# Turning nine blocks of tokens on VectorE, and moving maxima, router and entries among the key pairs

## The chip, the cores and the metric

The kernel runs on one core of one Trainium2 chip. The metric is the device time of one execution in microseconds (us), the median of several runs. A difference within 0.2% is about what can't be told from no change here.

## The reference

One layer on x of 4096 tokens by 256, all in float32: causal attention with one head, then a mixture of experts, each behind a layer norm and each added to x.

```python
x = x + attn(layernorm(x))      # softmax(mask(Q K^T / 16)) V, causal, S = 4096, D = 256
h = layernorm(x) @ W_in + b_in
probs = softmax(h @ W_gate + b_gate)          # 8 experts, the best 2 of each token
mid = relu(einsum('nd,edh->neh', h, W1) + b1) # hidden size 1024
moe = sum over a token's 2 experts of share * (mid @ W2 + b2)
x = x + moe @ W_out + b_out
```

## The kernel before

**Blocks of tokens.** The tokens are cut in eight blocks of 512 (`b`, `TB`), each of four tiles of 128, and in sixteen groups of 256 queries (`g`, two a block). `xb[b]` holds x of a block in SBUF from the first load to the end; attention is added to it in place, later b_out.

**Turning.** A matrix product on TensorE wants the channel on the partitions. So each block is turned twice: its normalized rows before attention (`z`, made by `ln_rows(0, b)`, turned into `zT[b]`), and its normalized rows after attention (`z1`, turned into `z1T`). `turn` (L263) does this with eight transposes of 128x128 on TensorE (line 268) into two banks of PSUM, and two copies of 128x512 out of them by VectorE (line 274). `squares` (L804) is another way that the kernel already has, for the rows of the experts: sixteen of VectorE's own 32-wide transposes straight from SBUF to SBUF (line 810).

**Attention.** `project(b)` makes qT of a block (`pq`) and `values(b)` its V with a column of ones (`pv`). `scores(g)` computes for each of the g+1 key pairs `c` (256 keys each) the scores of 256 queries (`ps`, line 484). ScalarE copies them out (line 493), VectorE keeps a running maximum over the pairs (`mx`, line 499). After the last pair, `top` is turned (`pt`, line 520), reduced to `m`, spread again (`pmax`, line 527), and then VectorE subtracts it from each pair (line 531) and ScalarE takes the exponential in place. `attend(g)` multiplies the result with the values (`po`, line 549), in two banks for the two tiles of 128 queries. Then VectorE divides by the sum (`rinv`, line 559), adds to x and takes the statistics for the second norm.

**The order in the loop.** Iteration g issues `scores(g + 1)` ahead of `attend(g)`, so that exponentials of the next group run beside the products of this one. At the first group of a block b the loop also prepares z of block b+1 and lets block b-1 enter the experts: `enter(b - 1)` turns z1, multiplies it with W_in and the gate (`ph`, line 291), and writes the rows to DRAM; `route(b - 1)` finds the two best experts on VectorE by a chain of some twenty small operations, counts tokens with two products on TensorE (`pk`, lines 349 and 352), and scatters the token's number into the expert's list in DRAM (`slots`, line 367, by GpSimd). At the end of `route`, GpSimd adds b_out to x of the block (line 386). The last block's first group (g = 14) differs: `enter(6)` stands inside `scores(15)` after `BETWEEN` pairs, and `plan` and `route(6)` follow.

**The experts.** Work items (full blocks `a` and `b` of 256 entries, halves `c`, quarters in pairs `d`, a late one `z`) fetch their slots, rows and weights some items ahead, multiply with W1 (`pm`) and W2 (`pe`), and scatter to `parts`. At the end the two parts of each token are added, multiplied with W_out (`pa`, `pf`) and added to x.

**Order.** A planner places the instructions of each engine by their data and their place in the source; `tc.keep_in_program_order` ties single ones to the order of the source. Each engine executes its own list in order. PSUM has four banks for scores and other products (`ps_mm`), two for `ps_tr`, two for sums (`ps_o`). SP's queue issues loads and stores, POOL's the indirect ones.

**The beginning.** Five products of zeros run while the first loads arrive (line 112). Q and K weights are turned and multiplied with each other (`pqk`, line 419); between the two halves of that product stands `turn` of block 0.

Of the kernel before, what the change touches and what calls it, by code (L numbers as in the profile page):

```python
# [26 lines left out]
TOPK = 2  # L27
SQ = 32
LATE = 2
USUAL = 6  # L30
BETWEEN = 6
# [4 lines left out]
def preln_attention_moe_kernel(  # L36
# [51 lines left out]
    dram = ctx.enter_context(tc.tile_pool(name="dram", bufs=1, space=bass.MemoryType.DRAM))  # L88
    psum = ctx.enter_context(tc.tile_pool(name="psum", bufs=1, space=bass.MemoryType.PSUM))
# [13 lines left out]
    slots = dram.tile([NE * R, 1], I32, name="slots")  # L103
# [6 lines left out]
    pw = ps_mm("warm")  # L110
    for _ in range(5):
        done = nc.tensor.matmul(
            pw[:, :QB],
            lhsT=zeros,
            rhs=zeros.unsqueeze(1).to_broadcast([P, QB // P, P]),
            start=True,
            stop=True,
        )
        tc.keep_in_program_order(done)
# [4 lines left out]
    def load_square(w, name, queue=nc.sync):  # L124
        t = const.tile([P, ND, w.shape[1]], F32, tag=name, name=name)
        queue.dma_start(out=t, in_=w.rearrange("(c p) e -> p c e", p=P))
        return t

# [6 lines left out]
    kw_sb = load_square(Kw, "kw", nc.scalar)  # L135
    qw_sb = load_square(Qw, "qw", nc.scalar)
# [104 lines left out]
    def ln_shift(k, b, tiles=TPB):  # L241
        s = ts(b, tiles)
        mv, rstd, shift = lns[k]
        nc.vector.scalar_tensor_tensor(
            shift[:, s, :], mv[:, s, 0:1], -1.0, rstd[:, s, :], ALU.mult, ALU.mult
        )

    def ln_rows(k, b, pool, tiles=TPB):

        mv, rstd, shift = lns[k]  # L250
        zs = []
        for j in range(TPB):
            t = b * TPB + j
            if t % tiles == 0:
                ln_shift(k, t // tiles, tiles)
            z = pool.tile([P, D], F32, tag=f"z{k}", name=f"z{k}_{t}", bufs=TPB)
            nc.vector.tensor_scalar(
                z, xb[b][:, j, :], rstd[:, t, :], shift[:, t, :], ALU.mult, ALU.add
            )
            zs.append(z)  # L260
        return zs

    def turn(k, b, zs, zT, first=False):  # L263

        for c in range(ND):
            pt = ps_mm(f"pz{k}_{b}_{c}")
            for j in range(TPB):
                done = nc.tensor.transpose(pt[:, ts(j, P)], zs[j][:, ts(c, P)], ident)
                if first:
                    tc.keep_in_program_order(done)  # L270
            if first and c:
                nc.scalar.copy(zT[:, c, :], pt)
            else:
                nc.vector.tensor_copy(zT[:, c, :], pt)
# [6 lines left out]
    def enter(b, zs, pool):  # L281

        zT = pool.tile([P, ND, TB], F32, tag="z1T", name=f"z1T{b}", bufs=1)
        turn(1, b, zs, zT)
# [3 lines left out]
        for j in range(TPB):  # L288
            ph = ps_mm(f"ph{b}_{j}")
            for c in range(ND):  # L290
                nc.tensor.matmul(
                    ph[:, :DG],
                    lhsT=zT[:, c, ts(j, P)],
                    rhs=win_sb[:, c, :],
                    start=(c == 0),
                    stop=(c == ND - 1),
                )
            nc.vector.tensor_tensor(lg[:, j, :], ph[:, D:DG], bgate_bc, ALU.add)
            nc.vector.tensor_tensor(hr[:, j, :], ph[:, :D], bin_bc, ALU.add)
# [12 lines left out]
    def route(b, lg, seen, pool):  # L312
# [34 lines left out]
        pk = ps_o(f"pk{b}")  # L347
        pkv = pk[:, : TPB * NE]
        nc.tensor.matmul(
            pkv, lhsT=before, rhs=both.rearrange("p t e -> p (t e)"), start=True, stop=False  # L350
        )
        nc.tensor.matmul(
# [6 lines left out]
        for k in range(TOPK):  # L359
# [6 lines left out]
            for j in range(TPB):  # L366
# [3 lines left out]
                    in_=assign[:, b * TPB + j, k : k + 1],  # L370
# [10 lines left out]
        for k in range(TOPK):  # L381
# [3 lines left out]

        nc.gpsimd.tensor_tensor(
            xb[b], xb[b], bout_bc.unsqueeze(1).to_broadcast([P, TPB, D]), ALU.add
        )
# [3 lines left out]
    attn = ctx.enter_context(tc.tile_pool(name="attn", bufs=1))  # L392
# [11 lines left out]
    def prepare_scores(between):  # L404

        wT = {}
        for name, w in (("qwT", qw_sb), ("kwT", kw_sb)):
            wT[name] = attn.tile([P, ND, D], F32, tag=name, name=name)
            pt = ps_tr(f"p{name}")
            for h in range(ND):  # L410
                for c in range(ND):
                    nc.tensor.transpose(pt[:, ts(h * ND + c, P)], w[:, c, ts(h, P)], ident)
            nc.scalar.copy(wT[name].rearrange("p h d -> p (h d)"), pt)
# [54 lines left out]
    def scores(g, between=None):  # L468


        b, q = divmod(g, QPB)
        ss, mx = [], None
        top = attn.tile([P, QB], F32, tag="top", name=f"top{g}", bufs=2)
        for c in range(g + 1):
            if between is not None and c == BETWEEN:
                between()
# [15 lines left out]
            if c < g:  # L492
# [3 lines left out]
                else:  # L496
                    old = mx
                    mx = attn.tile([P, TB], F32, tag="mx", name=f"mx{g}_{c}", bufs=2)
                    nc.vector.tensor_tensor(mx, ps, old, ALU.max)  # L499
# [13 lines left out]
            for u in range(1, KU):  # L513
                nc.vector.tensor_tensor(
                    top[:, u * P :], top[:, u * P :], s[:, u, u * P :], ALU.max
                )

        pt = ps_tr(f"pt{g}")
        for u in range(KU):
            nc.tensor.transpose(pt[:, ts(u, P)], top[:, ts(u, P)], ident)  # L520
        m = attn.tile([P, KU], F32, tag="m", name=f"m{g}", bufs=2)
        nc.vector.tensor_reduce(
            m, pt[:, :QB].rearrange("p (u k) -> p u k", k=P), AX.X, ALU.max
        )
        pm = ps_tr(f"pmax{g}")
        for u in range(KU):
            nc.tensor.transpose(pm[:, ts(u, P)], m[:, u : u + 1].to_broadcast([P, P]), ident)  # L527
        for c in range(g + 1):
            s = ss[c]
            if c < g:  # L530
                nc.vector.tensor_tensor(  # L531
                    s, s, pm[:, :QB].unsqueeze(1).to_broadcast([P, KU, QB]), ALU.subtract
                )
                nc.scalar.activation(s, s, AF.Exp)  # L534
                continue
            for u in range(KU):
                nc.vector.tensor_tensor(
                    s[:, u, u * P :], s[:, u, u * P :], pm[:, u * P : QB], ALU.subtract
                )
                nc.scalar.activation(s[:, u, u * P :], s[:, u, u * P :], AF.Exp)  # L540
        return ss

    def attend(g, ss):
        po = [ps_o(f"po{g}_{u}") for u in range(KU)]
        for c in range(g + 1):
            for k in range(KU):
                kt = c * KU + k
                for u in range(k if c == g else 0, KU):
# [6 lines left out]
                    )  # L555
        for u in range(KU):
# [109 lines left out]
    def take_late():  # L666
# [8 lines left out]
        where = slots[ds(at, SB), :].rearrange("(p u) o -> p (u o)", u=SU)  # L675
# [29 lines left out]
    def fetch_rows(item):  # L705
# [8 lines left out]
        for j in range(parties):  # L714
# [9 lines left out]
                in_=slots[ds(at, su * rest), :].rearrange("(p u) o -> p (u o)", u=su),  # L724
# [25 lines left out]
    def fetch_weights(item, homes=None):  # L750
# [3 lines left out]
        sets, c2 = [], attn.tile([P, D], F32, tag="z0", name=f"c2_{k}{m}", bufs=TPB)  # L754
# [49 lines left out]
    def squares(to, of):  # L804


        for f in range(P // SQ):
            for q in range(P // SQ):
                pin(
                    nc.vector.transpose(  # L810
                        to[ts(f, SQ)][..., ts(q, SQ)], of[ts(q, SQ)][..., ts(f, SQ)]
                    )
                )

    def turn_rows(item, h):
# [4 lines left out]
        squares(  # L820
            hT.rearrange("p c (u s) -> p c u s", u=su),
            h.rearrange("p u (c f) -> p c u f", c=ND),
        )
# [115 lines left out]
    first_rows = ln_rows(0, 0, attn, 1)  # L939
    prepare_scores(lambda: turn(0, 0, first_rows, zT[0], True))  # L940
# [11 lines left out]
    for e in range(NE):  # L952
# [11 lines left out]
    assign = const.tile([P, NT, TOPK], I32, tag="assign", name="assign")  # L964
    nc.gpsimd.iota(assign, [[TOPK * P, NT], [1, TOPK]], base=0, channel_multiplier=TOPK)
    empty = attn.tile([P, NE * R // P], I32, tag="s", name="empty", bufs=NS)
    nc.gpsimd.memset(empty, NONE)
    nc.sync.dma_start(out=slots.rearrange("(p n) o -> p (n o)", p=P), in_=empty)
# [4 lines left out]
        out=rows[TOPK * (S - TB) :, :].rearrange("(t p) d -> p t d", p=P),  # L973
        in_=zero.unsqueeze(1).to_broadcast([P, TOPK * (TPB + 1), D]),
    )

    row = scores(0)
    values(0)
    prepare_biases()
    for g in range(NT // KU):  # L980
        b, q = divmod(g, QPB)
        coming = q == 0 and b + 1 < NB
        lg = []

        def send():
            lg.append(enter(b - 1, rows1, attn))


        last = q == 0 and b == NB - 1
        nxt = None  # L990
        if g + 1 < NT // KU:
            nxt = scores(g + 1, send if last else None)
        if coming:
            ahead = ln_rows(0, b + 1, attn)
        if last:
# [3 lines left out]
            seen = route(b - 1, lg[0], seen, attn)  # L999
            got, hTs = {}, {}  # L1000
            for n in range(AHEAD + 1):
                got[n] = fetch_rows(work[n])
            for n in range(AHEAD):
                got[n] += fetch_weights(work[n])
            weighed = AHEAD
        elif q == 0 and b > 0:
            send()
        if coming:
            turn(0, b + 1, ahead, zT[b + 1])
        attend(g, row)  # L1010
        row = nxt
        if coming:
            project(b + 1)
            values(b + 1)
        if lg and not last:
            seen = route(b - 1, lg[0], seen, attn)
        if q == QPB - 1:
            ln_rstd(1, b)
            if b + 2 < NB:
                stats0(b + 2)  # L1020
            rows1 = ln_rows(1, b, attn)
# [77 lines left out]
    for n, item in enumerate(work):  # L1099
# [13 lines left out]
        while weighed < len(work) and sum(map(sets_of, work[n : weighed + 1])) <= HOMES:  # L1113
# [3 lines left out]
            weighed += 1  # L1117
        following = None
        if n + 2 < len(work):
            following, behind = hidden(work[n + 1], got[n + 1], hTs.pop(n + 1), behind)  # L1120
        if n == 0:
            lg = enter(NB - 1, rows1, attn)
# [71 lines left out]
```

## Time and profile before

| what | value |
|---|---|
| median of 3 runs | 1090.61 us (1090.59 to 1092.51) |
| profiled execution: its time, its span | 1100.16 us, 1098.4 us |
| mean granted TensorE clock | 0.995 |
| TensorE (PE) busy | 1080.9 us, 98% |
| VectorE (DVE) busy | 689.2 us, 63% |
| ScalarE (ACT) busy | 331.9 us, 30% |
| GpSimd (POOL) busy | 238.1 us, 22% |
| attention, about | to 588 us |
| experts and last product, about | from 588 us |

The page is of one execution. Each row of a group of instructions gives its line, engine, operation, out<-in with shapes and the number of records, then busy time, mean duration in ns, and the idle time just before with what ended it. A float32 product appears as two records on PE, a transpose as one. Durations of neighbouring instructions can overlap, so what one costs its engine is read from start to start.

### The profile page before, as it was taken

The numbers are of one execution on the slowest core, as the hardware profiler recorded it, in microseconds if no ns is written. First come the engines' busy times: TensorE is split into PE (matmuls) and PEld (weight loads), VectorE is DVE, ScalarE is ACT, GpSimd is POOL, SyncE is SP. The second block draws the span as 40 slices with busy tenths as digits, with TensorE's granted clock in tenths as the row PEclk, the third lists the DMA queues.
The fourth block names the chain that finished last, engine by engine and source line by source line (L and its number), as shares of the span: only waits on it lengthen the run. The fifth ranks groups of instructions, "written<-read, shape, count | busy, mean of one in ns | idle before, by whom it ended". The sixth has DMA issues, their size and how long they took to land. (4 is left out here: it accounts for less than half of the span.)

```text
span 1098.4 us, 15700 instructions
## 1 busy us (share of the span) xinstructions
PE 1080.9 (98%) x5077; PEld 894.7 (81%) x5077; DVE 689.2 (63%) x2134; ACT 331.9 (30%) x731; POOL 238.1 (22%) x292
## 2 busy tenths in 40 slices
PE   7999999999999999999999989999999999999998
PEld 5878888888888888888888878687877777777887
DVE  4678576583673556346392643767778876868636
ACT  1323232332341423233132122232322332324244
POOL 2023211202102010201322412323232231313110
PEclk8999999999999999999999999999999999999999
DMA  8010101010001001001085465696969797979285
GB/s 265 2 40 1 39 0 39 1 39 1 1 1 39 1 1 39 1 1 39 4 260 174 133 187 186 222 337 220 339 209 351 233 330 219 339 214 316 99 289 190
DMA packets 114888, 148.34 MB, mean 135 GB/s; under 512 B 23149, under 2 KB 94770, under 8 KB 114804
## 3 DMA queue, kind: packets, MB, share of 16 engines
q1 hardware_dynamic: 105876, 129.70, 36.2%
q0 software_dynamic: 8384, 17.09, 4.6%
q8 instruction: 41, 0.67, 0.3%
q10 hardware_dynamic: 544, 0.52, 0.1%
q14 instruction: 43, 0.35, 0.1%
HBM read 124.79 MB, written 22.75 MB: 134 GB/s over the span
## 5 line engine op out<-in xcount | busy, mean ns | idle before, releaser
L549 PE MATMUL po<-v,s 128*128 128x257 f32 x1056 | 237.4, 380 | 1.1 <-DVE rinv L559 1.1
L484 PE MATMUL ps<-qT,zT 128*128 128x256 f32 x1088 | 233.0, 374 | 0.0
L484 PEld LDWEIGHTS ps<-qT,zT 128*128 128x128 f32 x1088 | 203.0, 190 | 27.8 <-issue 0.5
L549 PEld LDWEIGHTS po<-v,s 128*128 128x128 f32 x1056 | 197.3, 190 | 28.0 <-issue 1.5
L493 ACT COPY s<-ps 128x512 f32<-128x512 f32 x120 | 70.2, 585 | 192.8 <-PE ps L484 140.1
L843 PE MATMUL pm_a<-hT_a,w_a 128*128 128x256 f32 x544 | 122.0, 383 | 2.9 <-ACT mid_a L852 2.9
L910 PE MATMUL pe_a<-w_a,mid_a 128*128 128x256 f32 x544 | 121.6, 380 | 0.0
L843 PEld LDWEIGHTS pm_a<-hT_a,w_a 128*128 128x128 f32 x544 | 104.4, 192 | 17.8 <-ACT mid_a L852 3.3
L910 PEld LDWEIGHTS pe_a<-w_a,mid_a 128*128 128x128 f32 x544 | 102.6, 190 | 19.0 <-issue 5.6
L367 POOL DMA_INDIRECT slots<-assign,ati x64 | 62.5, 977 | 254.8 <-DVE ati L365 236.4
L852 ACT ACTIVATE mid_a<-pm_a,c_a 128x256 f32<-128x256 f32 x136 | 63.9, 472 | 171.0 <-PE pm_a L843 144.9
L499 DVE TENSOR_TENSOR mx<-ps,mx 128x512 f32<-128x512 f32 x91 | 62.8, 690 | 83.0 <-ACT s L493 61.5
L534 ACT ACTIVATE s<-s 128x512 f32<-128x512 f32 x120 | 71.7, 629 | 59.5 <-DVE s L531 59.2
L810 DVE STREAM_TRANSPOSE hT_a<-h_a 32x128 f32<-32x128 f32 x272 | 82.2, 302 | 6.3 <-issue 2.5
L531 DVE TENSOR_TENSOR s<-s,pmax 128x512 f32<-128x512 f32 x120 | 73.0, 679 | 4.9 <-PE pmax L527 4.9
L919 POOL DMA_INDIRECT parts<-y_a,slot_a x34 | 34.0, 1001 | 170.0 <-DVE y_a L918 149.9
L810 DVE STREAM_TRANSPOSE mid_c<-raw_c 32x256 f32<-32x256 f32 x128 | 55.8, 436 | 1.9
L910 PE MATMUL pe_b<-w_b,mid_b 128*128 128x256 f32 x256 | 56.8, 380 | 0.0
L843 PE MATMUL pm_b<-hT_b,w_b 128*128 128x256 f32 x256 | 56.6, 379 | 0.0
L910 PEld LDWEIGHTS pe_b<-w_b,mid_b 128*128 128x128 f32 x256 | 48.5, 190 | 9.4 <-issue 2.8
L843 PEld LDWEIGHTS pm_b<-hT_b,w_b 128*128 128x128 f32 x256 | 48.6, 190 | 6.6
L852 ACT ACTIVATE mid_b<-pm_b,c_b 128x256 f32<-128x256 f32 x64 | 30.1, 470 | 63.0 <-PE pm_b L843 62.2
(280 smaller groups left out, 1211.4 us busy)
## 6 DMA issues: line engine op xcount, KB each, us to landing
w_a<-in_L_ffn_W_dram SPq DMA_DIRECT2D x68, 512.0 KB
w_d<-in_L_ffn_W_dram SPq DMA_DIRECT2D x48, 512.0 KB
w_c<-in_L_ffn_W_dram SPq DMA_DIRECT2D x32, 512.0 KB
w_b<-in_L_ffn_W_dram SPq DMA_DIRECT2D x32, 512.0 KB
rows<-hr SPq DMA_DIRECT2D x16, 512.0 KB
yp<-parts SPq DMA_DIRECT2D x14, 512.0 KB
x<-in_L_attn_x_dram SPq DMA_DIRECT2D x7, 512.0 KB
out_dram<-ot SPq DMA_DIRECT2D x14, 256.0 KB
```

What stands on the lines that cost most here:

```text
L367: put = nc.gpsimd.indirect_dma_start(out=slots, out_offset=bass.IndirectOffsetOnAxis(ap=ati[:, j : j + 1], axis=0), in_=assign[:, b * TPB ...
L484: nc.tensor.matmul(ps[:, u * QB + lo : (u + 1) * QB], lhsT=zT[kt // TPB][:, d, ts(kt % TPB, P)], rhs=qT[b][:, d, q * QB + lo : (q + 1) * Q ...
L493: nc.scalar.copy(flat, ps)
L499: nc.vector.tensor_tensor(mx, ps, old, ALU.max)
L531: nc.vector.tensor_tensor(s, s, pm[:, :QB].unsqueeze(1).to_broadcast([P, KU, QB]), ALU.subtract)
L534: nc.scalar.activation(s, s, AF.Exp)
L549: nc.tensor.matmul(po[u][:, : D + 1], lhsT=ss[c][:, k, ts(u, P)], rhs=vb[kt // TPB][:, kt % TPB, :], start=(kt == 0), stop=(kt == g * KU + u),
L810: nc.vector.transpose(to[ts(f, SQ)][..., ts(q, SQ)], of[ts(q, SQ)][..., ts(f, SQ)])
L843: nc.tensor.matmul(pm[:, :SB], lhsT=w1[c][:, ts(f, P)], rhs=hT[:, c, :], start=(c == 0), stop=(c == ND - 1),)
L852: nc.scalar.activation(mid[f // 2][:, f % 2, :], pm[:, :SB], AF.Relu, bias=c1[:, f : f + 1])
L910: nc.tensor.matmul(pe[ts(j, rest), :D], lhsT=mid[f][:, ts(u, P)][:, ts(j, rest)], rhs=w2[f // (NF // 2)][:, f % (NF // 2), :], start=(f == 0),
L919: put = nc.gpsimd.indirect_dma_start(out=parts, out_offset=bass.IndirectOffsetOnAxis(ap=slot[:, u : u + 1], axis=0), in_=y[:, u, :], in_of ...
```

## The change

- z of blocks 4 to 7 and z1 of blocks 2 to 6 are turned by VectorE: `TURNED` gives the first of each. Normalization and turn become a list of small steps, `fill`, that `scores(g + 1)` spreads behind its running maxima, tied to that order. Blocks 0 to 3 and z1 of blocks 0, 1 and 7 are turned by TensorE as before.
- Statistics and z of block b+2 come at the end of the first group of block b; before, the statistics came at the end of the second group and z during the next first one.
- `scores` returns the rest of its work as `finish` (turning the maxima, subtraction, exponentials). From g = 4 on it stands in `attend(g)` after pair min(g - 2, 4). `enter` of blocks 2 to 6 stands after pair 5. In g = 14 the first weights are issued after pair 6 and `route(6)` after pair 11.
- The sums of the last group take banks of `ps_mm`.
- Four more products of zeros stand ahead of the first turn, whose transposes go by tile.
- The source adds b_out during work items 4 to 11.
- A slot in DRAM takes a line of 16 numbers in place of one; its filling at the beginning and the zeroed rows (two blocks in place of one) grow accordingly.
- The weights of Q and K, their turned forms and the biases `c2` share a pool of four buffers; z of a block is one tile.

The core of the diff:

```diff
-BETWEEN = 6
+CALM = 4
+TURNED = (4, 2)
...
+    def squares_todo(to, of):
+        return [
+            partial(nc.vector.transpose, to[ts(f, SQ)][..., ts(q, SQ)], of[ts(q, SQ)][..., ts(f, SQ)])
+            for f in range(P // SQ)
+            for q in range(P // SQ)
+        ]
+    def rows_todo(hT, h):
+        return squares_todo(
+            hT.rearrange("p c (u s) -> p c u s", s=P), h.rearrange("p u (c f) -> p c u f", f=P)
         )
...
-                    nc.vector.tensor_tensor(mx, ps, old, ALU.max)
+                    done = nc.vector.tensor_tensor(mx, ps, old, ALU.max)
+                    for do in fill[len(fill) * (c - 1) // parts_of : len(fill) * c // parts_of]:
+                        tc.keep_in_program_order(done)
+                        done = do()
...
-    def attend(g, ss):
-        po = [ps_o(f"po{g}_{u}") for u in range(KU)]
+    def attend(g, ss, between):
+        home = ps_mm if g == NT // KU - 1 else ps_o
+        po = [home(f"po{g}_{u}") for u in range(KU)]
...
+            for do in between.get(c, ()):
+                do()
...
+    def turn_first():
+        warm(4, ps_o("warm2"))
+        turn(0, 0, first_rows, zT[0], True)
...
+            nxt, finish = scores(g + 1, fill)
+            if g < CALM:
+                finish()
+            else:
+                between[min(g - 2, 4)] = [partial(finish, True)]
+        fill = []
...
+            if b - 1 < TURNED[1]:
+                turn(1, b - 1, rows1, z1T)
+                send()
+            else:
+                between[5] = [partial(send, True)]
...
+            between[6], between[11] = [fetch_first], [find]
...
+        if q == 0 and b + 2 < NB:
+            stats0(b + 2)
+            by_dve = b + 2 >= TURNED[0]
+            ahead = ln_rows(0, b + 2, fill if by_dve else None)
+            if by_dve:
+                fill += rows_todo(zT[b + 2], ahead)
         if q == QPB - 1:
             ln_rstd(1, b)
-            rows1 = ln_rows(1, b, attn)
+            by_dve = TURNED[1] <= b < NB - 1
+            rows1 = ln_rows(1, b, fill if by_dve else None)
+            if by_dve:
+                fill += rows_todo(z1T, rows1)
...
+        if AHEAD < n <= AHEAD + NB:
+            xr = xb[n - AHEAD - 1]
+            nc.gpsimd.tensor_tensor(
+                xr, xr, bout_bc.unsqueeze(1).to_broadcast([P, TPB, D]), ALU.add
+            )
```

## The prediction

> **What bounds the kernel now.** I read the busy shares first, then TensorE's waits, then its timeline, and last the granted clock in short stretches.
>
> ```profile
> span 1098.4 us, 15700 instructions
> ...
> PE 1080.9 (98%) x5077; PEld 894.7 (81%) x5077; DVE 689.2 (63%) x2134; ACT 331.9 (30%) x731; POOL 238.1 (22%) x292
> ...
> L268 PE MATMUL pz<-ident,z 128*128 128x128 f32 x128 | 18.9, 285 | 3.7 <-DVE z L257 3.7
> ```
>
> TensorE (PE) has work in flight for 98% of the span. What TensorE no longer has to do comes off the time; what any other engine does counts only where TensorE waits for it. Its waits are few:
>
> ```profile
> PE pz L268 <- DVE z L257: 3.7, 3, 2.8
> PE pm_a L843 <- ACT mid_a L852: 2.9, 1, 2.9
> PE pt L520 <- DVE top L512: 1.6, 2, 1.2
> PE po L549 <- DVE rinv L559: 1.1, 1, 1.1
> ```
>
> The timeline gives the price of the work that goes:
>
> ```profile
> 31.76 1.04 PE L268 MATMUL pz<-ident,z 128*128 128x128 f32 x8
> 32.63 1.47 PE L549 MATMUL po<-v,s 128*128 128x257 f32 x6
> ...
> 59.89 0.33 PE L520 MATMUL pt<-ident,top 128*128 128x128 f32 x1 [1.25 <-DVE top L512]
> ```
>
> Eight transposes hold TensorE from 31.76 to 32.63: 0.87 us, 0.109 each. One 128x257 product (two records) takes 0.434 us, from start to start in the same timeline; a key pair of scores (eight records of 128x256 at 0.216) 1.73.
>
> **The transposes of nine blocks.** Of sixteen blocks turned (z and z1 of eight blocks), z of blocks 4 to 7 and z1 of blocks 2 to 6 leave TensorE: 9 x 8 = 72 transposes, 72 x 0.109 = **-7.8 us**. Above, the row's busy time allows 18.9/128 = 0.148 each, 10.6 us; below, nothing, if TensorE merely waits instead. I take 7.8, as back to back starts are what the next product sees.
>
> VectorE (DVE) gets nine times sixteen transposes of 32x256 and loses eighteen copies of 128x512:
>
> ```profile
> L810 DVE STREAM_TRANSPOSE mid_c<-raw_c 32x256 f32<-32x256 f32 x128 | 55.8, 436 | 1.9
> ...
> L244 DVE SCALAR_TENSOR_TENSOR ln0shift<-ln0mv,ln0rstd 128x4 f32<-128x4 f32 x7 | 10.7, 1535 | 0.5 <-POOL ln0rstd L239 0.5
> ...
> L244 DVE SCALAR_TENSOR_TENSOR ln1shift<-ln1mv,ln1rstd 128x4 f32<-128x4 f32 x8 | 1.3, 163 | 4.8 <-POOL ln1rstd L239 4.8
> ```
>
> 144 x 0.436 = 62.8, less 18 x 0.684 (the row of z1T's copies) = 12.3: +50.5 us, 740 of 1098. This is free as long as its stage covers it. The tightest is the first: block 4, filled into scores(6). There VectorE has a shift 0.16, four normalizations of 0.41, sixteen transposes 7.0 and five maxima of 0.69: 12.3 us, from 3.5 us after the scores begin (two key pairs), then mask and maxima of the diagonal, 1.8: ready at 17.6. TensorE needs 6 x 1.73 + 1.3 = 11.7 for these scores, then, because the transposes of the maxima (pt) now stand behind fourteen products of attend(5), 14 x 0.434 = 6.1: it arrives at 17.8. Cover 0.2 us; without the move of the maxima it would be gone by 6. In scores(7) VectorE starts late (4.2 us in) and ends at 18.6 against 22.5; from 8 on pairs and cover grow. The four banks of scores hold: a bank is wanted again four pairs (6.9 us) later, while VectorE falls behind by at most 2.5 - 1.73 = 0.8 us a pair.
>
> The two shift rows, same size, 1.54 against 0.16 us, show VectorE held up while GpSimd (POOL) adds b_out (2.36 us each). The source moves that add to the experts' items, but the scheduled order of POOL still has it in the attention stage, only ahead of the next blocks' rstd instead of behind it. There VectorE does maxima out of PSUM and 32-wide transposes, and those kept their 0.69 and 0.30 us beside such an add in this trace: the hold of some 1.4 us a block goes from VectorE.
>
> **The early stalls.** The wait of 1.25 at 59.89 is for a maximum that took 2.0 us beside such an add. The add now starts behind the normalizations, two maxima before it: I take -1.0. The product pq of block 2 waited 0.35 for its turned rows; the turn now stands ahead of ten products: -0.3. Together **-1.3**, between 0 and -2.
>
> **The beginning.** Four more warming products (eight records) stand in the gap before the first transposes.
>
> ```profile
> 7.90:11.30 3.40, 0.61 (x4) 1.00 1.10 326
> 11.30:14.70 3.40, 2.50 (x9) 0.50 1.09 353
> 14.70:18.20 3.50, 3.50 (x8) 0.51 1.08 350
> 18.20:21.60 3.40, 3.40 (x11) 1.00 1.10 375
> ```
>
> Columns: stretch and length, PE's busy time, granted clock, DMA share, GB/s. After a stretch with 0.61 us of work the clock is halved for two stretches. There five transposes, two products of qk and the first four records of pq run at half speed: 5 x 0.11 + 4 x 0.22 + 4 x 0.43, at most 3.1, of which waits for z cover some 0.7: 2.4. With eight records more (8 x 0.216 = 1.7) the first stretch has 2.3 us of work. The row says that a stretch so filled keeps the clock (4.5 to 7.9, with about 2.4 us of work, half of it transposes, was followed by 1.00): gain 2.4. [...] I take **-1.5**, between. The warming ends near 10.2, before z at 11.24, so it delays nothing; at half clock (3.5 us) it would cost 0.7.
>
> **The last sums.** attend(15) takes banks of the scores' pool, so it no longer waits for block 14's sums to leave: the 1.1 us row, **-1.1**. The first experts' products find two of those four banks in use, but want the third only 1.7 us later, when VectorE (0.16 + 0.47 behind the end) has freed it.
>
> **What now waits.** The entries of blocks 2 to 6 (ph) and the maxima move into attend; the number of products is the same. But the router of a block now stands on VectorE behind the subtractions of the maxima and the sums of attend, and TensorE's counting products (pk) keep their place behind pq and pv; behind pk stand all later scores. From the first sum's reciprocal to pk TensorE needs 0.87 + 8 x 0.432 + 16 x 0.217 = 7.8 us. VectorE has in this stretch two sums, four statistics, two copies of qT and the router:
>
> ```profile
> 174.38 0.19 DVE L331 TENSOR_TENSOR hot<-left,top 128x32 f32<-128x32 f32 x1
> 174.49 0.16 DVE L379 TENSOR_TENSOR tot<-top,top 128x4 f32<-128x4 f32 x1
> 174.60 0.19 DVE L332 TENSOR_TENSOR hot<-hot,rank 128x32 f32<-128x32 f32 x1
> ```
>
> Starts are 0.11 apart where the next does not need the last, 0.22 where it does. Laid out in the new order with these steps (0.6 a copy, 0.4 a sum or statistic with its aggregate) the chain ends 7.0 to 7.5 us behind: even with TensorE. The same for block 6, whose pk now stands in attend(15): 16.3 us behind the maxima for TensorE, 16.8 for VectorE. Five places, each even within half a microsecond: I take 0.3 each, **+1.5**; 0 to 5 in all.
>
> **At no cost.** The rows of `hr` for block 6 pass behind the weights of items a0 and a1 on SP; a2's weights, next behind them, wait for buffers of attend(15) anyway. Lines of 64 bytes leave POOL's 64 scatters at their 0.98 us; the table's longer filling and more zero rows add 3.1 MB behind the loads of x, when DMA is all but idle (slice two of the page: 2 GB/s), some 10 us that nothing waits for. Slot loads become 4-byte pieces, four items ahead.
>
> **Sum.** -7.8 - 1.3 - 1.5 - 1.1 + 1.5 = -10.2. The profiled execution took 1100.16 (span 1098.4) and would take 1090.0; it is 9.5 us above the median of the runs, 4.6 of that perhaps the wait at 632 (2.9) and the half clock behind it, which the change does not touch. Against the median: 1090.61 - 10.2 = **1080.4**.
>
> **Rivals.** (1) *The router is late*, which ends slower. If the small operations cost their full 0.19 and statistics 0.4 plus 0.17, the chain to pk ends at 18.6 instead of 16.4 after the maxima in blocks 3 to 5, 2.3 to 2.9 us late, at five places 12 to 14 us: 1090.6 - 11.7 + 14 = 1093. It decides from 2.3 us a place. For it: the order on VectorE has it directly behind other work. Against: starts 0.11 apart. (2) *VectorE is the bound in the turned pairs*: 0.6 us a transpose instead of 0.436 makes scores(6) 2.4 us late and takes some of 7's cover; with half-late routers, 1085. For: cover of 0.2. Against: the same form has 128 records at 0.436. (3) *More comes off*: 0.148 a transpose, the full clock, all early stalls, no new wait: -10.6 - 2.4 - 1.1 - 2 = 1074.5. [...] Against: 0.87 a group wherever it was not waiting. (4) *The chain is hidden anyway*: TensorE waits where it had transposed, within 2 us of before; against it stands the 98%.
>
> **How the numbers follow.** My forecast 0.69, rival 2 0.14, rival 3 0.07, rival 1 0.05, rival 4 0.05. A change under 0.2% (2.2 us) can't be told from none here. Faster 0.90, same 0.05, slower 0.05. The range leaves out rival 1, 4 and the far half of 3: 1076 to 1086, which takes in the ends of the unknown terms (7.8 and 10.6; 0.7 and 2.4; 0 and 5).
>
> **What would show it.** PE's `pz` row with 56 records in place of 128 and PE busy near 1070; 144 new stream transposes near 0.43; the `ln0shift` row near 0.2; no wait of `po` on `rinv`; clock 1.0 from 11 to 15 us. Wrong would be: waits of `pk` on `both` or `past`, or of `pt` on `top`, of over 2 us together.

## The result, and the profile after

| | before | after |
|---|---|---|
| median, series of the result | 1090.60 us (6 runs, 1090.13 to 1092.51) | 1081.07 us (6 runs, 1081.01 to 1081.33) |
| ratio, 95% interval | | 0.991 (0.990 to 0.992) |
| profiled execution: time, span | 1100.16, 1098.4 us | 1081.01, 1079.2 us |
| median, series of the experiments | 1097.7 to 1098.6 us (11 to 23 runs) | 1087.64 us (4 runs, 1086.62 to 1090.23) |
| ratio there | | 0.9901 (0.9873 to 0.9929) |

The change makes the kernel 9.5 us faster; 1080.4 was forecast. In the experiments both kernels took some 7 us more than in the series of the result, with the same ratio. So times are compared inside one series only, and kernels of different series by their ratio to the kernel before.

The profile of the changed kernel, its head and the groups that the prediction named (columns as before):

```profile
span 1079.2 us, 15699 instructions
...
PE 1069.7 (99%) x5013; PEld 889.7 (82%) x5013; DVE 728.9 (68%) x2260; ACT 332.2 (31%) x731; POOL 238.4 (22%) x293
```

```profile
L534 DVE STREAM_TRANSPOSE z1T<-z 32x256 f32<-32x256 f32 x80 | 34.9, 436 | 1.7
L534 DVE STREAM_TRANSPOSE zT<-z 32x256 f32<-32x256 f32 x64 | 27.9, 436 | 1.3
L287 PE MATMUL pz<-ident,z 128*128 128x128 f32 x56 | 7.5, 274 | 0.1
L259 DVE SCALAR_TENSOR_TENSOR ln0shift<-ln0mv,ln0rstd 128x4 f32<-128x4 f32 (+1 forms) x11 | 1.8, 165 | 4.9 <-POOL ln0rstd L250 4.9
```

TensorE has 56 transposes of rows instead of 128; VectorE has 144 new ones, at 436 ns each. The shift, 1.54 us before, takes 0.165. In the profile before, five of the seven larger shifts started inside GpSimd's addition of b_out and took 2.08 to 2.09 us each, the others 0.15 to 0.17; after, none stands beside it. VectorE's 728.9 us are 11 below the forecast 740; 9.6 of that are these shifts. TensorE's waits in the same profile (us in total, times, longest):

```profile
PE ph L323 <- DVE z1T L294: 1.2, 1, 1.2
PE pk L384 <- DVE both L375: 1.1, 1, 1.1
...
PE ph L323 <- DVE z1T L534: 0.3, 1, 0.3
PE pk L389 <- DVE past L379: 0.3, 1, 0.3
```

The waits for `z`, `top`, `rinv` and `mid_a` are gone from the list, and one for `both`, which the earlier page did not have, is there. The start, in stretches (length, PE's busy time, granted clock, DMA share, GB/s):

```profile
7.90:11.30 3.40, 3.23 (x17) 1.00 1.09 329
11.30:14.70 3.40, 3.31 (x14) 1.00 1.10 352
14.70:18.20 3.50, 3.50 (x15) 1.00 1.10 350
```

From 11.3 to 18.2 us the clock is 1.00, where it was 0.50 and 0.51.

**An account of TensorE's time.** To see where the gain comes from, each distance between the starts of two successive TensorE records was split in two: what the record's passes take back to back (256 columns 0.216 us, a transpose 0.108), and the rest, called lost: waits, half clock, and small gaps. The column "passes" is the sum of the first part; the others hold the lost time between the stated places of the span. Every kernel here loses 5.2 us from 650 us on, and has 4.6 us ahead of its first record and behind the start of its last; with these each line adds up to the span. All in us:

```
                               passes  0-20  20-160  160-500  500-570  570-650   span
before (first profile)         1059.2  10.5    7.7     2.2      2.4      6.6    1098.4
after  (first profile)         1053.2   4.7    5.1     1.7      3.0      1.8    1079.2
before, in the experiments     1059.2   9.4    7.8     2.2      2.4      6.5    1097.2
after, in the experiments      1053.2   4.8    5.2     1.7      5.4      6.5    1086.6
maxima ahead                   1053.2   5.0    9.7     9.5      3.7      6.4    1097.2
turned twice                   1053.2   4.8   12.6    16.1      3.8      7.5    1107.7
turned on TensorE              1060.9   6.2    5.1    10.6      1.7      6.4    1100.7
transposes beside              1060.9   4.8    5.4     1.5      1.9      4.9    1089.1
slots of 4 bytes               1053.2   4.7    5.0     1.7      5.2      6.5    1086.2
sums in two banks              1053.2   4.7    5.1     1.7      5.4      4.8    1084.8
no warming (second)            1051.4   8.2    5.1     1.8      3.7      6.5    1086.5
router of block 6 later        1053.2   5.0    5.1     1.7      2.6      4.8    1082.3
```

The passes fall by 7.8 for 72 transposes and rise by 1.7 for eight warming records. The column 570-650 holds one wait of 2.9 us (for `mid_a`, below), which the first profile of the change happens not to have; that, and not the change, makes 4.8 of the 19.2 us between the two first profiles, whose runs lie only 9.5 apart. The two profiles in the experiments both have it and lie 10.6 us apart. Between the two profiles of the change, 7.4 us apart, 4.7 lie in this column and 2.4 in the one before it.

Of the kernel before there is no profile of an execution at its 1090.6 us. So it is the 10.6 us that are taken apart here, and the 9.5 only as far as they are alike.

### The profile page after: what moved, and what is told of

Its sections match the earlier page's. It is cut to its first block, busy times and chain, and to the rows that moved or that the text cites. A ratio compares the mean times of both kernels' runs of the same rounds, so it can differ in the third digit from the quotient of the medians.

```text
span 1079.2 us, 15699 instructions
## 1 busy us (share of the span) xinstructions
PE 1069.7 (99%) x5013; PEld 889.7 (82%) x5013; DVE 728.9 (68%) x2260; ACT 332.2 (31%) x731; POOL 238.4 (22%) x293
```

## The experiments

**The kernel before, profiled again.** No edit.

> The kernel before, profiled a second time. Its first profile took 1100.16 us where the runs took 1090.6. Theory: the extra 9.5 us belong to that one execution (the wait of 2.9 us at 632 with half clock behind it, and half clock from 11.3 to 18.1). Then this profile has a span near 1088.8, no wait over 1 us between experts' products, and less half clock at the beginning. Rival: they belong to the kernel and the profile's own load; then the span is near 1098 again with the same waits.

It took 1099.0 us (one run, span 1097.2) beside a median of 1097.7. The theory failed: the same wait for `mid_a` of 2.8 us stands at 631 us, with half the clock behind it, and the clock is halved at the beginning too, for one stretch instead of two (0.50 from 13.0 to 16.4 us; the mean granted clock of the execution is 0.997). So this is no accident of the first profile. TensorE's longest waits in this profile:

```profile
PE pz L268 <- DVE z L257: 3.3, 3, 2.2
PE pm_a L843 <- ACT mid_a L852: 2.8, 1, 2.8
PE pt L520 <- DVE top L512: 1.6, 2, 1.2
PE po L549 <- DVE rinv L559: 1.1, 1, 1.1
```

**The changed kernel again, as control.** No edit.

> The changed kernel itself, unedited, as the control for the kernels beside it. Both theories: 10 us under the kernel before of the same chip, ratio 0.991. The prediction's steps say its waits for both and past stay under 2 us together and the wait for pm_a on mid_a stays away, as in the profile of the change. The rival (the wait for pm_a belongs to the chip, not to the kernel) says that 2.8 us show up at 615 to 635 us, with half the clock behind it.

1087.64 us against 1098.15, ratio 0.9901. Two of its waits are longer than in the first profile, in the same view:

```profile
PE pm_a L881 <- ACT mid_a L890: 2.8, 1, 2.8
PE pk L384 <- DVE both L375: 1.9, 1, 1.9
```

The expectation drawn from the first profile (`mid_a` away) was wrong, the rival right: the wait is here with both kernels, at the same place in the program. The waits for `both` and `past` (0.3) are 2.2 us together and so just over the 2 us that were expected at most.

**The price of 72 transposes.** First all blocks were turned on TensorE again, the rest left as changed:

```diff
-                between[5] = [partial(send, True)]
+                between[5] = [partial(turn, 1, b - 1, rows1, z1T), partial(send, True)]
...
-        elif q == 0 and b + 1 < TURNED[0]:
+        elif q == 0 and b + 1 < NB:
...
+            by_dve = False
```

(the last line at both places).

> The changed kernel with all sixteen blocks turned by TensorE, the rest of the change kept (maxima, entries and router among the pairs, early z). By the prediction's step 72 transposes of 0.109 us come back: slower by 7.8 us, near 1088.9, PE with 128 transposes, and VectorE some 50 us less busy. Rival, 0.148 each: slower by 10.6. Rival, that the gain came from the other parts and TensorE only waited less: within 2 us of 1081.1.

1100.00 us (20 runs), ratio 1.0023 (1.0014 to 1.0032): slower than before, and by the ratios some 13 us behind the change, where 7.8 or 10.6 were expected. Its waits and its line of the account (8.9 us more lost in 160-500) show that this is not the price of transposes alone:

```profile
PE ph L323 <- ACT s L581: 2.8, 2, 2.5
PE pk L384 <- DVE both L375: 2.1, 2, 1.1
```

Entries and routers wait anew. So a second kernel leaves VectorE alone and issues the 72 transposes on TensorE besides, into banks that nobody reads:

```diff
+    def spare(k, b, z):
+        pts = [ps_mm(f"pz{k}_{b}_{c}") for c in range(ND)]
+        for c in range(ND):
+            for j in range(TPB):
+                nc.tensor.transpose(pts[c][:, ts(j, P)], z[:, j, ts(c, P)], ident)
```

> The changed kernel with the 72 transposes issued on TensorE as well, where they stood, into banks of the scores' pool, and nobody reads them; VectorE's work stays as changed, and the output is the same. This is the price of the transposes alone. The prediction's step (0.109 each, start to start) says 7.8 us slower than the change. Rival, by the busy time of the row (0.148 each): 10.6 us. The earlier kernel that turned all blocks on TensorE took 12 to 13 us more than the change; if transposes alone cost that, it shows here too; if its own waits (2.8 for ph, 3.1 for pk, half clock) made the rest, 7.8 is seen here.

1092.55 us (6 runs, 1090.92 to 1094.25), 4.6 us above its neighbour with narrow slots (1087.96), which stands for the change in this series. That is neither 7.8 nor 10.6. The account of the two profiles, whose spans differ by 2.9 us, tells why: the passes are 7.8 us more (72 x 0.108), and the lost time is 4.9 less. The eight of one turn, in the timeline (start, busy):

```profile
166.12 1.04 PE L300 MATMUL pz<-ident,z 128*128 128x128 f32 x8
166.99 2.39 PE L329 MATMUL ph<-win,z1T 128*128 128x264 f32 x10
```

From their start to the next they take 0.87 us, the 8 x 0.109 of the prediction, as seven of the nine such groups do; one took 1.16 and one is split by a product, into halves of 0.44. What went the other way is in the columns 500-570 and 570-650: in this kernel the order on VectorE came out otherwise, `pk` hardly waited for `both` (0.07), and in the profiled run the clock was never halved (mean granted clock 1.000). The price of 7.8 rests on these starts; the times of the runs alone don't show it.

**The maxima back ahead of attend.**

```diff
-CALM = 4
+CALM = 99
```

> The transposes of the maxima put back ahead of the middle of attend in all pairs (they stand behind 6 to 9 products instead of 16 to 20 in scores 6 to 12). The prediction's step (cover of 0.2 us that the move alone provides, gone by 6 without it) says that TensorE waits for top: 2.0 us in scores(6), 2.1 in (7), 1.1 in (8), 0.8 in (9): 4 to 6 us slower than the change, with waits of pt on top in the profile. Rival: VectorE and TensorE overlap enough without it, so within 1 us of the change.

1100.89 us (20 runs, 1098.92 to 1104.06), ratio 1.0026 (1.0018 to 1.0034): 13.3 us slower than the control (10.6 by the spans of the two profiles), more than the expected 4 to 6, and slower than the kernel before. The wait is the one named, in the list of waits:

```profile
PE pt L558 <- DVE top L549: 8.1, 6, 2.2
```

By the account 2.3, 2.4, 1.8, 1.3 and 0.9 us are lost in scores(6) to (10), 8.7 in all, where 2.0, 2.1, 1.1, 0.8 and nothing were expected. Half the clock behind the second of them (0.50 from 163.0 to 166.4 us) adds 1.7, and smaller waits some 2; at `pk` of block 6 this profile loses 1.7 less than the control (column 500-570). The same place of scores(6), here and in the profile after:

```profile
130.08 4.07 PE L593 MATMUL po<-v,s 128*128 128x257 f32 x18
136.32 0.65 PE L558 MATMUL pt<-ident,top 128*128 128x128 f32 x2 [2.17 <-DVE top L549]
```

```profile
130.22 7.11 PE L593 MATMUL po<-v,s 128*128 128x257 f32 x32
137.17 0.38 PE L558 MATMUL pt<-ident,top 128*128 128x128 f32 x2
```

The maximum of the latter, on VectorE:

```profile
136.45 0.29 DVE L551 TENSOR_TENSOR top<-top,s 128x128 f32<-128x128 f32 x1
```

Nine products (18 records) stand ahead of the transposes in the one, sixteen in the other, and there the maximum is ready 0.4 us early. Without the move of the maxima, taking the transposes from TensorE gains nothing; and the kernel turned on TensorE, which has the move without the taking, gains nothing either. In these kernels the two edits are worth something together only.

**Turned twice.** Each of the nine blocks is turned twice on VectorE, with the same result:

```diff
-                fill += rows_todo(zT[b + 2], ahead)
+                fill += 2 * rows_todo(zT[b + 2], ahead)
...
-                fill += rows_todo(z1T, rows1)
+                fill += 2 * rows_todo(z1T, rows1)
```

> Each of the nine turned blocks is turned twice on VectorE (16 stream transposes of 0.436 more a block, 63 us more of VectorE in all), output the same. The prediction's cover (0.2 us in scores 6, 3.9 in 7, growing with the pairs) says waits of 6.0 in scores(6), 3.5 in (7), 2.1 in (8), 1.7 in (9) and nothing later, 10 to 16 us slower than the change. Rival (VectorE is never near the bound): within 3 us of the change.

1107.75 us, 20.1 above the control (the spans: 21.1). Its longest wait, and the first of its places, in scores(6):

```profile
PE pt L558 <- DVE top L549: 12.0, 5, 4.2
```

```profile
130.41 9.28 PE L593 MATMUL po<-v,s 128*128 128x257 f32 x42
143.86 0.80 PE L558 MATMUL pt<-ident,top 128*128 128x128 f32 x2 [4.17 <-DVE top L549]
```

By the account 4.3, 3.6, 2.5, 1.7 and 0.7 are lost in scores(6) to (10), 12.8 against the expected 13.3: right in sum, too high in the first. There 21 products (42 records) stand ahead of the transposes in place of the changed kernel's 16, 2.2 us more cover: 7.0 of added transposes less 0.4 and 2.2 is 4.4. The time is above the expected 10 to 16 because the clock is halved in five stretches behind such waits, another 1.7 us each (mean granted clock 0.991, against 0.997 in the control). VectorE is near the bound where the prediction put it.

**No warming**, in both series:

```diff
     def turn_first():
-        warm(4, ps_o("warm2"))
```

> The changed kernel without its four additional products of zeros. By the prediction's step the clock is halved behind the gap: slower by 1.5 us (0.7 to 2.4), near 1082.6, with half clock granted in the profile between 11 and 18 us. Rival: the profile of before caught a rare execution and the clock mostly holds across the gap; then within 0.3 us of 1081.1.

> The four warming products left out again, now beside the unedited changed kernel. The prediction's term says 0.7 to 2.4 us slower than the change, taken 1.5. Rival: 1.7 us of TensorE work goes and nothing comes back, so within 0.3 us of the change, or faster where the clock is halved anyway.

1089.09 us (ratio 0.992, 0.9904 to 0.9937), and 1088.41 us beside the control's 1087.64: 0.8 us slower, with runs that overlap. The times alone show no loss for certain. The first 20 us show it better: 3.4 us more lost in the second profile, 3.0 in the first, for 1.7 us of passes less, so warming gains 1.3 to 1.7. In the second profile the clock, in the columns of the stretches above:

```profile
9.10:12.50 3.40, 1.92 (x10) 1.00 1.09 356
12.50:16.00 3.50, 3.50 (x8) 0.51 1.09 348
```

The spans are equal (1086.5, 1086.6) because this profile lost no half clock at `pk` of block 6, and the control's did (0.50 from 548.9 to 552.3 us; column 500-570: 3.7 and 5.4).

**The last sums back in their two banks.**

```diff
-        home = ps_mm if g == NT // KU - 1 else ps_o
+        home = ps_o
```

> The changed kernel with the sums of the last group in the two banks of the other groups. By the prediction's step TensorE waits for the division of group 14: slower by 1.1 us, a wait of the sums on rinv near 548 us. Rival, that VectorE is later there than before since it now also turns rows of the experts and routes: slower by 2 to 4.

1086.58 us (ratio 0.9897, 0.988 to 0.9913; the control's is 0.9901): no loss is seen, neither the 1.1 nor the rival's 2 to 4, though the intervals are too wide to rule out 1.1. The profile decides. Its list of waits has no `pk` of this size, but

```profile
PE po L593 <- DVE hot L366: 1.9, 1, 1.9
```

```profile
545.75 0.48 DVE L607 SCALAR_TENSOR_TENSOR x<-po,rinv,x 128x256 f32<-128x256 f32 x1
...
546.37 3.19 PE L593 MATMUL po<-v,s 128*128 128x257 f32 x8 [1.92 <-DVE hot L366]
```

The view names `hot`, which ended last; the bank itself is read by `x<-po`, which ended 0.1 us earlier. The last attend waits for its banks for as long as it otherwise waits for the router (column 500-570: 5.4 in both). VectorE is late, and TensorE meets it at whichever of the two comes first.

**Slot entries of 4 bytes.** `LINE = 1` instead of 16 and the table filled as before.

> Entries of the slot table back at 4 bytes, filled as in the kernel before, all else as changed. The prediction's step (64 byte lines cost and bring nothing) says within 0.5 us of the change, ratio to before 0.990. Rival: the width of the scattered lines has to do with the wait of pm_a on mid_a during the last scatters; then the wait of 2.8 us is longer or shorter by a microsecond or more, and the time with it.

1087.96 us, ratio 0.9897 (0.9882 to 0.9911). By the ratios that is 0.4 us under the control, within the noise: no cost or gain of the wider lines is seen, and the wait for `mid_a` is 2.8 us as with the others.

**The router of block 6 later.** The wait of 1.9 is the change's own. VectorE's timeline of the control, from the end of the subtractions to `both`:

```profile
543.39 0.19 DVE L368 TENSOR_REDUCE best<-hot 128x4 f32<-128x32 f32 x1
543.61 0.30 DVE L861 STREAM_TRANSPOSE hT_a<-h_a 32x128 f32<-32x128 f32 x1
543.94 0.19 DVE L369 TENSOR_TENSOR hot<-hot,best 128x32 f32<-128x32 f32 x1
544.16 0.30 DVE L861 STREAM_TRANSPOSE hT_a<-h_a 32x128 f32<-32x128 f32 x1
544.50 0.19 DVE L372 SCALAR_TENSOR_TENSOR left<-hot,prob 128x32 f32<-128x32 f32 x1
545.34 0.17 DVE L605 RECIPROCAL rinv<-po 128x1 f32<-128x1 f32 x1 [0.65 <-PE po L593]
...
547.96 0.19 DVE L375 TENSOR_TENSOR both<-hot,hot 128x32 f32<-128x32 f32 x1
```

Between the steps of the router stand the transposes of the first expert's rows (`hT_a`), some ten of 0.30 us, so that a step takes 0.55 instead of 0.22. And VectorE stands idle for 0.65 us ahead of `rinv`, for the sum of attend(14). From the router's first operation to the end of `both` it takes 7.55 us here, 6.82 in the first profile of the change (the same ten transposes, no such idle time), and 4.81 in both profiles of the kernel before, which has none of the transposes in between. The edit issues the router behind the third pair of attend(15):

```diff
-            between[6], between[11] = [fetch_first], [find]
+            between[6] = [fetch_first]
...
+        if g == NT // KU - 1:
+            between[2] = [find]
         attend(g, row, between)
```

(and ties the product in front to the source's order). It does not shorten the router; it makes TensorE come for its result later.

> The router of block 6 is issued inside the products of attend(15), behind its third key pair, so that its counting products (pk) stand behind 12 products of attend(15) instead of 4: 8 x 0.434 = 3.5 us later for TensorE. The theory that the new wait of pk on both (1.9 us in the control, then half the clock) is what the change loses there says 2 to 3.5 us faster than the change, about 0.988 of before. Rival: VectorE's chain is put off as well (two sums of attend(14) pass ahead of it, some 1.2 us) or the places that come out of it are wanted later by the planning of the experts, so within 0.5 us of the change.

1085.39 us (4 runs, 1084.07 to 1086.34), ratio 0.9882 (0.9868 to 0.9896), 2.6 us under its neighbour with narrow slots, as expected. The account has it in the column 500-570: 2.6 against 5.2, of which 1.7 is the half clock. The wait for `both` is gone, of `pk` there remains, by the waits of this kernel,

```profile
PE ph L323 <- DVE z1T L294: 1.2, 1, 1.2
PE pk L389 <- DVE past L379: 1.1, 2, 0.8
```

**And the first entries inside attend.** In addition, `send()` of blocks 0 and 1 goes to `between[0]`.

> As the kernel with the later router of block 6, and the entries (ph) of blocks 0 and 1 issued behind the first key pair of attend instead of directly behind their turned rows. The wait of ph on z1T at 53 us (1.2, lost 1.36 with its start) should go: 1.0 to 1.4 us faster than the kernel before it in this list. Rival: the routers of these blocks come later, pk waits for both instead, no gain.

1084.43 us (4 runs, 1083.44 to 1086.53), ratio 0.9876 (0.9861 to 0.9891): the fastest here, 3.2 us under the control. Against the kernel before it the median is 1.0 us lower, but the runs overlap and the spans differ by 0.3. The wait of `ph` is gone and a shorter one of the next turn, for the same copies, has come:

```profile
PE pz L287 <- DVE z1T L294: 0.8, 1, 0.8
```

So the expected 1.0 to 1.4 is not shown; of the two edits the later router is the one whose gain is.

## Why the prediction was right

The time was right (1080.4 against 1081.07), the sum (-10.2 against -9.5 and -10.5), and the main term. That the sum came out so close is in part luck: two terms were too small by 2.7 us together, and the end of attention was wrong by as much the other way. By the two profiles of the experiments:

| step | predicted | measured | by |
|---|---|---|---|
| 72 transposes | -7.8 | -7.8 | passes; transposes beside |
| early stalls | -1.3 (0 to -2) | -2.6 | column 20-160 |
| beginning | -1.5 (0.7 to 2.4) | -2.9 | column 0-20, less 1.7 of warming |
| last sums | -1.1 | 0 | sums in two banks |
| new waits of routers | +1.5 (0 to 5) | +3.0 | column 500-570 |
| other | 0 | -0.3 | 160-500 and 570-650 |
| sum | -10.2 | -10.6 | spans |

**Transposes, and their cover.** Right, both: 0.109 each, start to start, and VectorE at the limit in scores(6). Cover there is 0.4 us (0.2 predicted, though with 14 products where 16 stand), 2.5 in scores(7) (3.9 predicted), and 4 to 5.5 from (8) to (12). That the move of the maxima makes this cover was shown by taking it away. Without it TensorE waits 2.3 us in scores(6), not 6: nine products then still stand ahead of the transposes.

**The early stalls.** The mechanism was right, the size too small. In the two profiles of the experiments `pt` loses 2.1 us less (1.0 forecast) and `pq` 0.6 less (0.3 forecast), `pz` 0.4 and `pmax` 0.3 less. Against that `ph` of block 0 waits 1.2 for its turned rows and `pk` of block 0 waits 0.3 for `past`, which the prediction did not have. No run took these apart.

**The beginning.** Warming alone gains 1.3 to 1.7, so the term was right. The other 1.2 us, which the kernel without warming also has, is a step that the prediction lacked. VectorE's statistics of the fourth tile of block 0, in the kernel before (again), in the one turned on TensorE, and in the control:

```profile
7.64 0.43 DVE L231 BATCH_NORM_STATS2 bn<-x 128x6 f32<-128x256 f32 x1 [1.38 <-DMA x<-in_L_attn_x_dram]
```

```profile
7.74 0.43 DVE L242 BATCH_NORM_STATS2 bn<-x 128x6 f32<-128x256 f32 x1 [1.43 <-DMA x<-in_L_attn_x_dram]
```

```profile
6.40 0.40 DVE L242 BATCH_NORM_STATS2 bn<-x 128x6 f32<-128x256 f32 x1
```

In the first two they wait for a load of x, and the last z of the block ends at 13.0 and 13.1 us; in the control they follow the third tile's at once, and z ends at 11.8. Both profiles of the kernel before and the kernel turned on TensorE have this wait, the other eleven profiles don't. It is not the order of the first transposes by tile: the kernel turned on TensorE has that order and the warming, and loses 6.2 us in the first 20, 1.4 more than the control. Why some of the kernels wait for this load is open. In the first profile of before the wait is 1.56 us, in that of the change there is none, and SyncE issues the four loads of block 0 from 0.75 us on in 1.83 us in the one, from 0.74 on in 1.82 in the other.

**The clock behind transposes.** The prediction took the middle of two ends: 2.4, if the clock stays behind the filled stretch, as it did in the kernel before behind 4.5 to 7.9 us, and 0.7, the author's estimate for a clock that drops again behind the next stretch (2.4 less the 4 x 0.43 of the slow `pq`). In the changed kernel the clock stayed: 1.00 in each stretch from 4.5 to 21.6 us of its first profile, and from 6.1 to 16.4 in the control. The stretch of the kernel before had 2.30 us of busy time (about 2.4 in the prediction); counted in passes (busy time overlaps) it held 1.8, of which 0.9 were products. What transposes alone do is not shown by the changed kernel's beginning, since its stretch from 10.7 to 14.1 has over 2 us of products.

**The last sums.** This step failed. The wait on `rinv` was real, but what it waited for, VectorE behind the last group, stays late; in other banks TensorE runs 4 products on and waits for `pk` instead. A wait removed is a gain only if the next thing from the same late engine comes in time.

**The routers.** The size failed, and so did the distribution. Five places of 0.3 were taken; in blocks 2 to 5 the control's `pk` waits 0.1 us in all. Block 6 alone waits 1.9, and loses 1.7 more where the clock is halved behind it (0.50 from 548.9 to 552.3 us). The step that failed is "16.3 us behind the maxima for TensorE, 16.8 for VectorE", half a microsecond late. Counted from the start of `m`, TensorE is due at `pk` after 17.2 us; VectorE is done with `both` after 18.2 in the first profile of the change and 19.0 in the control, so 1.1 and 1.9 late. The prediction counted the router's own operations and left out the ten `hT_a` transposes among them (0.33 from start to start, 3.3 us) and, in the control, the 0.65 of idle time ahead of `rinv`. No run took the transposes out, so that the chain would be in time without them is not shown. The rival of the late router (2.3 us and more at five places) took place at one. With `past` and `pt` (0.2) the control's waits come to 2.4 us, and so pass the 2 us that the prediction had named as a sign of being wrong.

**At no cost.** For the slot lines no cost is seen (4 bytes: within 0.4 us). The held-up VectorE did go: 0.165 us a shift. One `top` of 128x256 still takes 1.2 us beside GpSimd's addition (0.42 elsewhere), and TensorE does not wait for it.

**The 9.5 us of the first profile of before.** The remark that 4.6 of them are perhaps the wait at 632 us and its half clock fits in size: 2.9 and 1.7 (a clock of 0.50 from 636.0 to 639.4 us). It comes with both kernels, and it makes the first two profiles look too far apart. What the other 4.9 are is open.

## What to carry to other kernels

Work moved to an engine with free time is free only as far as the next reader stands late enough: move the reader first (here the maxima, 10.6 us by the profiles and 13 by the runs), then the work. To tell whether a chain on another engine is in time, list everything that the engine's order puts between its steps, not the chain alone. And when a wait goes, look for the next result of the same late engine before booking the gain.

## What the runs showed of the hardware

**One wait, with half the clock behind it and without.** The wait for `mid_a` is 2.8 us in the control and with the later router. In the control 0.61 us of TensorE's busy time stand in the 3.4 us about it, and the next 3.4 are granted 0.50; with the later router 1.66 and 2.33 us stand in two stretches, and the clock is 1.00 (columns as above; control first):

```profile
620.60:624.00 3.40, 0.61 (x4) 0.99 0.35 95
624.00:627.40 3.40, 3.40 (x10) 0.50 0.65 177
```

```profile
616.50:619.90 3.40, 1.66 (x8) 1.00 0.19 47
619.90:623.30 3.40, 2.33 (x11) 1.00 0.63 192
```

In 3.4 us at 0.50 TensorE does the work of 1.7 us at 1.00, so 1.7 are lost, an estimate from these two numbers. The control's wait of 1.9 for `both` left 1.53 us of busy time in 545.5 to 548.9, and 0.50 followed; one of 1.6 in the kernel with the maxima ahead left 1.81 in 200.6 to 204.0, and 1.00 followed. Busy time alone does not sort them: the 1.66 of the later router was followed by 1.00, and 1.92 without warming, from 9.1 us on in the second profile, by 0.51. The time of one program goes with the clock from run to run: the kernel turned on TensorE took 1097.7 to 1099.0 us in the five runs with mean clock 1.000, and 1102.4 to 1102.7 in the four with 0.995.

**A stretch with transposes.** In the kernel with the first entries inside attend the stretch from 52.3 to 55.7 held, counted in passes, 1.28 us of transposes and 0.43 of products, and the clock stayed at 1.00:

```profile
52.30:55.70 3.40, 2.33 (x15) 1.00 0.00 0
55.70:59.10 3.40, 3.40 (x19) 1.00 0.00 0
```

No run changed the transposes of such a stretch alone, so what they did for the clock is not shown.

**A wait of 2.9 us that stays open.** It is in 13 of the 14 profiles, with both kernels, and not in the first profile of the change. ScalarE starts `mid_a` of an item 5.9 us behind the first product of `pm_a` (control, at 623.1 us; 1.1 in the first profile of the change), and at the same time SyncE's two weight transfers take three times as long to issue. SyncE's queue in the first profile of the change, then in the control:

```profile
613.04 2.11 SPq L832 DMA_DIRECT2D w_a<-in_L_ffn_W_dram  x2
```

```profile
615.85 6.10 SPq L832 DMA_DIRECT2D w_a<-in_L_ffn_W_dram  x2
```

VectorE's small operations have gaps there too (the longest 1.9 us). GpSimd issues its eight slot scatters from 610.2 to 620.1 us in the control, across most of this; in the first profile of the change it does so from 607.5 to 617.5, across the 2.11 us of the same transfers too. With lines of 4 bytes in place of 64 the wait is 2.8 us as well. Why is not known, and nothing here tells it.
